# First stage of a cross-attention and expert kernel: a sum moved into PSUM, a norm moved to GpSimd, compares moved between VectorE's statistics

## The chip, the cores and the metric

The kernel runs on one core of a Trainium2 chip. The metric is the device time of one execution in microseconds (us). Before the change three runs took 929.35, 930.76 and 930.84 us, median 930.76.

A core has five engines that work at the same time, each through its own instructions in order: TensorE (PE in the profile: matrix products into PSUM; its weight loads are shown apart as PEld), VectorE (DVE), ScalarE (ACT: functions such as logarithm and exponential, also copies), GpSimd (POOL) and SyncE (SP: issues most DMAs here). An engine waits on a semaphore when its next instruction needs something that isn't there yet, and everything behind that instruction waits with it.

## What is computed

The reference is one transformer-like layer pair over `x` (32 x 56 x 256) and a context `ctx` (32 x 1500 x 256), all float32. Cut to what matters here:

```python
# first attention: a decayed scan over the context, averaged to one row per batch
s_t = K * s_{t-1} + (ctx_t @ W_in.T + b_in)         # K = sigmoid(decay)
summary = mean_t(s_t @ W_out.T + b_out)             # one row of 256 per batch
y  = layernorm(x) + summary
x  = x + (y - mean(y)) / sqrt(var(y) + eps) * gamma + beta
# first expert layer: 16 experts, the best 6 of each token
h = layernorm(x)
scores = softmax(h @ gate_w.T)
topk_w, topk_idx = top_k(scores, 6)
x = x + sum_e topk_w[e] * (silu(h @ wg[e].T) * (h @ wu[e].T)) @ wd[e].T
# second attention over ctx with a mask, then a layer of two experts
x = x + softmax(layernorm(x) @ ctx.T / 16, masked) @ ctx
x = x + top1_expert(layernorm(x))
return x
```

The change lies in the first stage: the first attention, the norm after it, the gate of the first expert layer, and the bookkeeping that sorts tokens by expert.

## The kernel before

The 32 batches are taken as 16 pairs (`NP = 16`). A pair's 2 x 56 tokens lie on the 128 partitions, batch 0 from partition 0 and batch 1 from partition 64, so that a pair is one tile of 128 x 256. The residual stream `xr` stays in SBUF for all pairs.

The context stands in a ring of five slots (`ring`, 1536 KB a batch). `load_ctx` (L145, issued by SP) fills a slot again as soon as `count_in` has read it.

The first stage's main loop is `for p in range(NP)` (L582). Its calls are written out by hand, and the order in which the calls stand is the order in which TensorE, VectorE, ScalarE and SP get their instructions; GpSimd's order is found by a scheduler. One round works on four pairs at once, each at another step:

- **Pair p, the summary.** `count_in` (L294) multiplies both batches' context by the scan's decay weights: 24 products of 32 columns each, accumulated in `acc`. `sum_out` (L408, ScalarE) copies it to SBUF; `sum_in_columns` (L414 on TensorE, L419 on VectorE) adds it up to columns, `sp` and then `sv`; `projected` (L427, then a ScalarE copy to `sm`, L431) applies the two weight matrices, multiplied beforehand; `to_rows` (L435) spreads the summary's rows over the 128 tokens, into `bp`.
- **Pair p-1, norms and gate.** `first_norm` adds `bp` to the normed input `zc` (L439), takes statistics (`stats`, L154 and L155) and lets ScalarE find the inverse root (`inverse_root`, L160 and L161: logarithm, then exponential). `residual` (L446, L447) applies it and takes the next statistics; `second_root` is the second inverse root; `second_norm` (L459, VectorE) makes the normed rows `xn`; `away` (L463, SP) stores them; `turned` (L166, L168) transposes them on TensorE and copies them to `xT`; `gate` (L471) gives 16 logits; `best` (a copy by ScalarE, L480, then L482 to L489 on VectorE, with an exponential, L491) marks the best six in `sel`.
- **Pair p-2, places.** `ranks` (L496, L497) counts, over tokens, how many chose each expert before; `counted` (L503, L504) turns that into positions; `places` (L510 to L526) splits a position into a block (`lvl`) and an offset (`off`), and prepares `vals`: the token's number and its weight for each expert and block. ScalarE makes the number half (L524). `ones_at` compares the offsets with 0 to 127, one 128 x 128 matrix per expert, 16 in all: twelve on VectorE in two instructions (L537, 1024 and 512 elements) and four on GpSimd (L543).
- **Pair p-3, sorting.** `sorted_in` (L562): 16 products on TensorE, of those matrices with `vals`, accumulated over all pairs in `owned`.

In every second round (p even, up to 12) `first_stats` (L393, L394 on VectorE and a root on ScalarE) and `first_rows` (L400, L404 on GpSimd: the normed input `zc`, and `beta` added to `xr`) prepare pairs p+2 and p+3.

In the order of before, `ones_at` stands at the end of a round, behind `best`, and `sorted_in` of the same pair follows in the next round. `first_stats` stands between `first_norm` and `residual`, `first_rows` behind `to_rows`. On TensorE a round is `count_in`, `sorted_in`, `ranks`, `sum_in_columns`, `turned`, `projected`, `gate`, `to_rows`. Six PSUM tiles a round go through a ring of five (`ps`).

After the loop, the last pairs are finished (L616 to L696) with `busy` (L552), products whose result nobody reads, in between; then the first expert layer begins with gathers of `xn` rows by GpSimd (L846).

Of the kernel before, what the change touches and what calls it, by code (L numbers as in the profile page):

```python
# [8 lines left out]
F32 = mybir.dt.float32  # L9
U8 = mybir.dt.uint8  # L10
I32 = mybir.dt.int32
AF = mybir.ActivationFunctionType
ALU = mybir.AluOpType
# [5 lines left out]
P = 128  # L19
B, S, D, T = 32, 56, 256, 1500  # L20
KD = D // P
NP = B // 2
# [6 lines left out]
NE = D // Q  # L29
CW = NCH * D  # L30
NRING, NXTRA = 5, 3
E0, F0, K0 = 16, 176, 6
# [22 lines left out]
def xattn_ffn_kernel(  # L55
# [94 lines left out]
    def stats(src):  # L150

        st = small.tile([P, 6], F32, tag="st", name="st")
        mv = small.tile([P, 4], F32, tag="mv", name="mv")
        V.bn_stats(out=st, in_=src)  # L154
        V.bn_aggr(out=mv[:, 0:2], in_=st)  # L155
        return mv
# [48 lines left out]
    with tc.tile_pool(name="p1", bufs=1) as p1, tc.tile_pool(name="p3", bufs=3) as p3, tc.tile_pool(  # L205
# [75 lines left out]
        def keep(p, **t):  # L281
            pend.setdefault(p, {}).update(t)

        def count_in(b):

            p, h = divmod(b, 2)
            if h == 0:
                keep(p, acc=psa.tile([P, 512], F32, tag="acc", name="acc"))
            acc = pend[p]["acc"]
            c = slots[b % NRING]  # L290
            for m in range(NCH // 4):
                for g in range(4):
                    j = 4 * m + g
                    PE.matmul(  # L294
                        acc[Q * g : Q * g + Q, 0:D],
                        lhsT=cz[:, j, 1 - h : 1 - h + Q], rhs=c[:, j, :],
                        start=(h == 0 and m == 0), stop=(h == 1 and m == NCH // 4 - 1),
                    )
            if b + NRING < B:
                load_ctx(b + NRING, c)  # L300
# [90 lines left out]
        def first_stats(o):  # L391
            for p in range(o, o + 2):
                V.bn_stats(out=st[:, p, :], in_=xr[:, p, :])  # L393
                V.bn_aggr(out=mva[:, p, :], in_=st[:, p, :])  # L394
            inverse_root(rsa[:, o : o + 2], mva[:, o : o + 2, 1])
# [10 lines left out]
        def sum_out(p):  # L406
            acc = p3.tile([P, D], F32, tag="acc", name="acc")
            A.copy(acc, pend[p]["acc"][:, 0:D])  # L408
            keep(p, acc=acc)

        def sum_in_columns(p):
            sp = ps.tile([P, 512], F32, tag="ps", name="sp")
            for k in range(KD):
                PE.matmul(  # L414
                    sp[:, 2 * k : 2 * k + 2], lhsT=pend[p]["acc"][:, k * P : (k + 1) * P],
                    rhs=sel2[:, 0:2], start=True, stop=True,
                )
            sv = p3.tile([P, KD, 2], F32, tag="sv", name="sv")
            V.tensor_scalar(  # L419
                sv.rearrange("p k h -> p (k h)"), sp[:, 0 : 2 * KD], 1.0 / T, None, ALU.mult  # L420
            )
            keep(p, sv=sv)

        def projected(p):
            sT = ps.tile([P, 512], F32, tag="ps", name="sT")
            for k in range(KD):
                PE.matmul(  # L427
                    sT[0:2, 0:D], lhsT=pend[p]["sv"][:, k, :], rhs=wc[:, k, :],
                    start=(k == 0), stop=(k == KD - 1),
                )  # L430
            A.copy(sm[0:2, :], sT[0:2, 0:D])  # L431

        def to_rows(p):
            bp = ps.tile([P, 512], F32, tag="ps", name="bp")
            PE.matmul(bp[:, 0:D], lhsT=takes, rhs=sm, start=True, stop=True)  # L435
            keep(p, bp=bp)

        def first_norm(p):
            V.tensor_tensor(zc[p], zc[p], pend[p]["bp"][:, 0:D], ALU.add)  # L439
            mv = stats(zc[p])  # L440
            inverse_root(mv[:, 2:3], mv[:, 1:2])
            keep(p, mv=mv)

        def residual(p):
            mv = pend[p]["mv"]
            V.scalar_tensor_tensor(zc[p], zc[p], mv[:, 0:1], gam, ALU.subtract, ALU.mult)  # L446
            V.scalar_tensor_tensor(  # L447
                xr[:, p, :], zc[p], mv[:, 2:3], xr[:, p, :], ALU.mult, ALU.add
            )
            keep(p, mv=stats(xr[:, p, :]))  # L450

        def second_root(p):
            mv = pend[p]["mv"]
            inverse_root(mv[:, 2:3], mv[:, 1:2])

        def second_norm(p):
            mv = pend[p]["mv"]
            xn = xnp.tile([P, D], F32, tag="xn", name="xn")
            V.tensor_scalar(xn, xr[:, p, :], mv[:, 0:1], mv[:, 2:3], ALU.subtract, ALU.mult)  # L459
            keep(p, xn=xn)  # L460

        def away(p):
# [37 lines left out]
        def counted(p):  # L500

            rk = pend[p]["rk"]
            V.tensor_tensor(pos[:, p, :], rk[:, 0:E0], base0, ALU.add)  # L503
            V.tensor_tensor(base0, base0, rk[:, E0 : 2 * E0], ALU.add)  # L504

        def places(p):

            nm, pr = pend[p]["nm"], pend[p]["pr"]
            qi = small.tile([P, E0], I32, tag="qi", name="qi")
            V.tensor_copy(qi, pos[:, p, :])  # L510
            V.tensor_scalar(qi, qi, 7, None, ALU.logical_shift_right)
            V.tensor_copy(lvl[:, p, :], qi)

            off = small.tile([P, E0], F32, tag="off", name="off")
            V.scalar_tensor_tensor(
                off, lvl[:, p, :], -float(P), pos[:, p, :], ALU.mult, ALU.add
            )
            V.scalar_tensor_tensor(off, off, 1.0, sel[:, p, :], ALU.add, ALU.mult)  # L518
            v = vals[:, p % 2]
            V.tensor_tensor(  # L520
                v[:, :, 1, :], e16.unsqueeze(1).to_broadcast([P, E0, NLP]),
                lvl[:, p, :].unsqueeze(2).to_broadcast([P, E0, NLP]), ALU.is_equal,
            )
            A.activation(v[:, :, 0, :], v[:, :, 1, :], AF.Copy, scale=ids[:, p : p + 1])  # L524
            V.reciprocal(nm[:, 1:2], nm[:, 1:2])
            V.scalar_tensor_tensor(  # L526
                v[:, :, 1, :], v[:, :, 1, :], nm[:, 1:2],
                pr.unsqueeze(2).to_broadcast([P, E0, NLP]), ALU.mult, ALU.mult,
            )
            keep(p, off=off)  # L530

        def ones_at(p):

            off = pend[p]["off"]
            hots = [at2.tile([P, NE, P], F32, tag="xq", name="oh") for h in range(2)]
            for h, n in ((0, NE), (1, NE // 2)):
                V.tensor_tensor(  # L537
                    hots[h][:, 0:n], iota.unsqueeze(1).to_broadcast([P, n, P]),
                    off[:, NE * h : NE * h + n].unsqueeze(2).to_broadcast([P, n, P]),
                    ALU.is_equal,  # L540
                )
            for i in range(NE // 2, NE):
                G.tensor_scalar(  # L543
                    hots[1][:, i, :], iota, off[:, NE + i : NE + i + 1], None, ALU.is_equal
                )
            keep(p, hots=hots)

        def busy(n):

# [32 lines left out]
        for p in range(NP):  # L582
            if p >= 1:
                first_norm(p - 1)
            if p % 2 == 0 and p + 2 < NP:
                first_stats(p + 2)
            if p >= 1:
                residual(p - 1)
                count_in(2 * p)
                second_root(p - 1)  # L590
                count_in(2 * p + 1)
            sum_out(p)
            if p >= 3:
                sorted_in(p - 3)
            if p >= 2:
                ranks(p - 2)
            if p >= 1:
                second_norm(p - 1)
                away(p - 1)
                some_pieces(1)  # L600
            sum_in_columns(p)
            if p >= 1:
                turned(p - 1)
            projected(p)
            if p >= 2:
                counted(p - 2)
                places(p - 2)
            if p >= 1:
                gate(p - 1)
            to_rows(p)  # L610
            if p % 2 == 0 and p + 2 < NP:
                first_rows(p + 2)
            if p >= 1:
                best(p - 1)
            if p >= 2:
                ones_at(p - 2)  # L616
            if p == NP - 3:
                load_w0_up()
            if p > NP - 3:
                some_pieces(6)  # L620
        first_norm(NP - 1)
        sorted_in(NP - 3)
        ranks(NP - 2)
        busy(2)
        residual(NP - 1)
        second_root(NP - 1)
        second_norm(NP - 1)
        away(NP - 1)
        some_pieces(len(pieces))
# [3 lines left out]
        gate(NP - 1)  # L633
        busy(1)
        best(NP - 1)
        ones_at(NP - 2)
        ranks(NP - 1)
        sorted_in(NP - 2)
        counted(NP - 1)
# [21 lines left out]
            )  # L661
        busy(2)
        places(NP - 1)
        ones_at(NP - 1)
        blk = p2.tile([P, 4], F32, name="blk")
        V.tensor_copy(blk, bp[:, 0:4])
        hot = slots[B % NRING].rearrange("p j d -> p (j d)")
# [704 lines left out]
```

## Time and profile before

| what | us |
|---|---|
| runs | 929.35, 930.76, 930.84; median 930.76 |
| the profiled execution, whole | 928.71 |
| its span | 927.0 |
| start of the span to the loop's first `first_norm` | 0 to 38.5 |
| loop, L439's first to last start | 38.5 to 200.1 |
| last pairs, to the first gather of the expert layer | 200.1 to 223.4 |
| the rest: both expert layers and the second attention | 223.4 to 927.0 |

Busy time of each engine by stretch of the span (us):

| stretch | length | PE | DVE | ACT | POOL | granted PE clock | DMA share | GB/s |
|---|---|---|---|---|---|---|---|---|
| 0 to 38 | 38.0 | 19.1 | 11.8 | 4.9 | 17.5 | 0.92 | 0.96 | 307 |
| 38 to 200 | 162.0 | 138.0 | 120.2 | 47.5 | 61.1 | 0.77 | 0.88 | 315 |
| 200 to 223.4 | 23.4 | 20.2 | 15.3 | 3.4 | 7.7 | 0.66 | 0.19 | 56 |
| 223.4 to 489 | 265.6 | 255.1 | 87.8 | 119.4 | 142.1 | 0.98 | 0.52 | 157 |
| 489 to 927 | 438.0 | 400.1 | 250.2 | 177.6 | 153.8 | 0.96 | 0.49 | 162 |

How to read the profile: the span is the time from the first to the last recorded instruction of one execution. A line of the timeline has start, duration, engine, line of the program, operation, what it writes `<-` what it reads, the shape, and how often it ran in a row; in brackets stand the idle time of the engine before it and who ended that. A line of the waits has who waited, for whom, and then the microseconds in total, the number of times and the longest. The granted clock is the share of its full clock that TensorE was given. Matmul ends are modelled, so a busy TensorE is not a TensorE at its peak.

### The profile page before, as it was taken

To read this page: it belongs to the slowest core of one execution; us is meant where nothing else is said; L and a number is where in the kernel's file an instruction comes from. 1 tells how busy PE (TensorE), PEld (TensorE's weight loads), DVE (VectorE), ACT (ScalarE), POOL (GpSimd) and SP (SyncE) were. 2 spreads that over 40 slices of the span, in tenths; PEclk is the share of its full clock that TensorE was granted. 3 is DMA by queue.
4 is the path that set the end of the run, shared out by engine and by line. 5 is a ranking of instruction groups with operands and counts; after the bars stand their busy time and mean duration, and the time that the engine had idled before them with its cause. 6 is when DMAs were issued, how large, how long until landed. Compare 5 with 4: busy or idle time off the path is not lost.

```text
span 927.0 us, 18683 instructions
## 1 busy us (share of the span) xinstructions
PE 832.5 (90%) x6664; PEld 539.8 (58%) x6664; DVE 485.3 (52%) x1409; ACT 352.8 (38%) x921; POOL 382.3 (41%) x464
## 2 busy tenths in 40 slices
PE   4698888887999898999996999987968989999997
PEld 4355444444777676777773566554635546666664
DVE  3377777774563222232227789977848533332222
ACT  0222222321444545444444575774734421111111
POOL 4333344335437545556633645664560321111110
PEclk9777777777999999999997999998998999999999
DMA  9998878881797624344537687888862911011110
GB/s 284 354 386 305 316 291 326 267 230 32 243 319 232 185 90 123 94 137 119 137 87 235 230 279 258 267 289 263 307 229 98 339 60 35 23 35 30 35 35 17
DMA packets 77820, 176.58 MB, mean 190 GB/s; under 512 B 7795, under 2 KB 41476, under 8 KB 77732
## 3 DMA queue, kind: packets, MB, share of 16 engines
q1 hardware_dynamic: 64756, 139.55, 43.7%
q0 software_dynamic: 12976, 35.85, 13.5%
q8 instruction: 56, 0.92, 0.4%
q14 instruction: 32, 0.26, 0.1%
HBM read 150.83 MB, written 25.20 MB: 190 GB/s over the span
## 4 chain that ended last, share of the span: by engine, by line
PE 44%; POOL 11%; DMA 9%; issue 6%; DVE 3%; ACT 2%; POOLq 0%; ACTq 0%; DVEq 0%
PE gu L714 22%; PE y L741 14%; DMA g<-ys,back 8%; POOL g L776 6%; PE tp L732 4%; PE tp L166 3%; POOL g L786 2%; PE op L1053 1%; DVE cT L966 1%; POOL g L788 1%; POOL g L787 1%; DMA xs<-pay,to 1%; PE sp L1005 1%; POOL xr L789 1%; POOL xs L1144 0%
## 5 line engine op out<-in xcount | busy, mean ns | idle before, releaser
L714 PE MATMUL gu<-w_sb,xT 128*128 x396 | 136.7, 467 | 8.8 <-ACT xT L168 7.6
L720 ACT ACTIVATE sg<-gu 128x176 f32<-128x176 f32 (+1 forms) x159 | 54.3, 342 | 216.7 <-PE gu L714 216.6
L846 POOL DMA_INDIRECT xb<-xn,idx x99 | 93.8, 947 | 100.1 <-PE tp L166 83.7
L726 DVE SCALAR_TENSOR_TENSOR hs<-sg,wgt,gu 128x176 f32<-128x176 f32 x99 | 39.3, 397 | 174.0 <-ACT sg L720 174.0
L714 PE MATMUL gu<-ring,xT 128*128 x240 | 114.2, 599 | 0.5 <-ACT xT L168 0.5
L776 POOL DMA_INDIRECT g<-ys,back x96 | 91.0, 948 | 33.2 <-issue 25.8
L741 PE MATMUL y<-w_sb,hT 88*128 x396 | 102.7, 382 | 0.0
L1005 PE MATMUL sp<-cT,xq 32*64 32x384 f32 x2048 | 94.2, 512 | 3.4 <-DVE cT L966 3.3
L714 PEld LDWEIGHTS gu<-w_sb,xT 128*128 128x128 f32 x396 | 74.8, 191 | 37.7 <-ACT xT L168 11.0
L724 DVE TENSOR_TENSOR hs<-sg,gu 128x256 f32<-128x256 f32 x60 | 25.2, 421 | 117.1 <-ACT sg L720 117.1
L966 DVE STREAM_TRANSPOSE cT<-ring 128x1536 f32<-128x1536 f32 x40 | 69.3, 1760 | 18.8 <-PE sp L1005 10.7
L732 PEld LDWEIGHTS tp<-ident,hs 128*88 128x88 f32 (+1 forms) x318 | 41.4, 131 | 63.2 <-issue 49.1
L1053 PE MATMUL op<-ring,pT 128*64 128x256 f32 x480 | 67.8, 396 | 9.2 <-issue 9.2
L543 POOL TENSOR_SCALAR oh<-iota,off 128x128 f32<-128x128 f32 x64 | 41.7, 665 | 80.3 <-DVE off L518 72.9
L1005 PEld LDWEIGHTS sp<-cT,xq 32*64 32x64 f32 x2048 | 45.4, 140 | 44.4 <-issue 17.6
L741 PEld LDWEIGHTS y<-w_sb,hT 88*128 88x128 f32 x396 | 67.9, 191 | 5.7 <-issue 0.2
L1307 POOL DMA_INDIRECT out<-ob,ti x15 | 14.8, 988 | 131.4 <-DVE ob L1304 131.4
L168 ACT COPY xT<-tp 128x256 f32<-128x256 f32 x130 | 48.4, 372 | 52.6 <-PE tp L166 51.6
L734 DVE COPY hT<-tp 88x256 f32<-88x256 f32 (+1 forms) x159 | 66.0, 415 | 0.6 <-PE tp L732 0.6
L714 PEld LDWEIGHTS gu<-ring,xT 128*128 128x128 f32 x240 | 45.6, 191 | 33.1 <-issue 29.4
L732 PE MATMUL tp<-ident,hs 128*88 128x128 f32 (+1 forms) x318 | 61.5, 276 | 2.6 <-DVE hs L724 2.6
L294 PE MATMUL acc<-ring,cz 128*32 128x256 f32 x768 | 62.9, 493 | 0.2 <-DVE cz L270 0.2
(258 smaller groups left out, 1361.2 us busy)
## 6 DMA issues: line engine op xcount, KB each, us to landing
ring<-in_cx SPq DMA_DIRECT2D x52, 1536.0 KB
extra<-in_cx SPq DMA_DIRECT2D x12, 1536.0 KB
ys<-yb SPq DMA_DIRECT2D x99, 128.0 KB
xs<-zrow SPq DMA_DIRECT2D x5, 771.0 KB
mu<-in_mask SPq DMA_DIRECT2D x16, 187.5 KB
w_sb<-in_wg SPq DMA_DIRECT2D x2, 1408.0 KB
w_sb<-in_wu SPq DMA_DIRECT2D x2, 1408.0 KB
xn<-xn SPq DMA_DIRECT2D x16, 128.0 KB
```

The lines of the kernel that those rows point to most:

```text
L168: A.copy(xT.rearrange("p k c -> p (k c)"), tp[:, 0 : KD * P])
L294: PE.matmul(acc[Q * g : Q * g + Q, 0:D], lhsT=cz[:, j, 1 - h : 1 - h + Q], rhs=c[:, j, :], start=(h == 0 and m == 0), stop=(h == 1 and m = ...
L714: PE.matmul(gu[:, 0 : 2 * fp], lhsT=xT[i][:, k, :], rhs=w[:, bass.ds(at[i] + (u * piece + k * 2 * fp), 2 * fp)], start=(k == 0), stop=(k = ...
L720: A.activation(sg, gu[:, 0:fp], AF.Silu)
L732: PE.transpose(tp[0:h, c * P : (c + 1) * P], a[:, c * h : (c + 1) * h], ident)
L734: V.tensor_copy(hT[i, u], tp[0:h, 0 : 2 * P])
L741: PE.matmul(y[i][:, 0:D], lhsT=a[:, c * P : (c + 1) * P], rhs=w[0:h, bass.ds(at[i] + (u * piece + doff + c * D), D)], start=(u == 0 and c ...
L776: G.indirect_dma_start(out=g[:, k, :], out_offset=None, in_=ys0[0 : n * P, :], in_offset=bass.IndirectOffsetOnAxis(ap=back[:, p, 3 * i + k ...
L846: G.indirect_dma_start(out=xb, out_offset=None, in_=xn0, in_offset=bass.IndirectOffsetOnAxis(ap=idx[:, i : i + 1], axis=0),)
L966: V.transpose(out=cT.rearrange("p j e q -> p j (e q)"), in_=slots[b % NS][:, :, P * n : P * n + P],)
L1005: PE.matmul(sps[a][64 * h : 64 * h + 64, 0 : Q * NCH], lhsT=xq[Q * a : Q * a + Q, e, 64 * h : 64 * h + 64], rhs=cTs[e // 4][h][Q * a : Q * ...
L1053: PE.matmul(op[64 * h : 64 * h + 64, 0:D], lhsT=pT[:, j, 64 * h : 64 * h + 64], rhs=slots[(2 * p + h) % NS][:, j, :], start=(j == 0), stop ...
```

## The change

1. The summary's rows are added to `zc` on TensorE: `to_rows` first multiplies `zc` by the identity into `bp`, then accumulates the rows on top. VectorE's add (L439) goes; the statistics and L446 read `bp` in PSUM.
2. `second_norm` runs on GpSimd, except for the last pair.
3. In `places`, ScalarE's scale (L524 before) stands after VectorE's product and works in place; the product no longer waits for it.
4. `ones_at` is split in two halves and moved by a round: for pair p-3, the first half behind `first_norm`, the second behind `residual`, in the round in which `sorted_in(p-3)` runs.
5. The order of the calls: `sum_out` before `second_root`; `counted` right behind `sum_in_columns`; `projected` before `turned`; `first_stats` from behind `first_norm` to behind `to_rows`; `first_rows` behind `best`.

```diff
         def to_rows(p):
             bp = ps.tile([P, 512], F32, tag="ps", name="bp")
-            PE.matmul(bp[:, 0:D], lhsT=takes, rhs=sm, start=True, stop=True)
+            PE.matmul(bp[:, 0:D], lhsT=ident, rhs=zc[p], start=True, stop=False)
+            PE.matmul(bp[:, 0:D], lhsT=takes, rhs=sm, start=False, stop=True)
             keep(p, bp=bp)
 
         def first_norm(p):
-            V.tensor_tensor(zc[p], zc[p], pend[p]["bp"][:, 0:D], ALU.add)
-            mv = stats(zc[p])
+            mv = stats(pend[p]["bp"][:, 0:D])
             inverse_root(mv[:, 2:3], mv[:, 1:2])
             keep(p, mv=mv)
 
         def residual(p):
             mv = pend[p]["mv"]
-            V.scalar_tensor_tensor(zc[p], zc[p], mv[:, 0:1], gam, ALU.subtract, ALU.mult)
+            V.scalar_tensor_tensor(
+                zc[p], pend[p]["bp"][:, 0:D], mv[:, 0:1], gam, ALU.subtract, ALU.mult
+            )
...
-            V.tensor_scalar(xn, xr[:, p, :], mv[:, 0:1], mv[:, 2:3], ALU.subtract, ALU.mult)
+            (V if p == NP - 1 else G).tensor_scalar(
+                xn, xr[:, p, :], mv[:, 0:1], mv[:, 2:3], ALU.subtract, ALU.mult
+            )
...
             V.tensor_tensor(
-                v[:, :, 1, :], e16.unsqueeze(1).to_broadcast([P, E0, NLP]),
+                v[:, :, 0, :], e16.unsqueeze(1).to_broadcast([P, E0, NLP]),
                 lvl[:, p, :].unsqueeze(2).to_broadcast([P, E0, NLP]), ALU.is_equal,
             )
-            A.activation(v[:, :, 0, :], v[:, :, 1, :], AF.Copy, scale=ids[:, p : p + 1])
             V.reciprocal(nm[:, 1:2], nm[:, 1:2])
             V.scalar_tensor_tensor(
-                v[:, :, 1, :], v[:, :, 1, :], nm[:, 1:2],
+                v[:, :, 1, :], v[:, :, 0, :], nm[:, 1:2],
                 pr.unsqueeze(2).to_broadcast([P, E0, NLP]), ALU.mult, ALU.mult,
             )
+            A.activation(v[:, :, 0, :], v[:, :, 0, :], AF.Copy, scale=ids[:, p : p + 1])
...
+        def ones_at(p, h):
+            off = pend[p]["off"][:, NE * h : NE * h + NE]
+            oh = at2.tile([P, NE, P], F32, tag="xq", name="oh")
+            n = NE // 2 if h else NE
+            V.tensor_tensor(
+                oh[:, 0:n], iota.unsqueeze(1).to_broadcast([P, n, P]),
+                off[:, 0:n].unsqueeze(2).to_broadcast([P, n, P]), ALU.is_equal,
+            )
+            for i in range(n, NE):
+                G.tensor_scalar(oh[:, i, :], iota, off[:, i : i + 1], None, ALU.is_equal)
+            pend[p].setdefault("hots", []).append(oh)
...
         for p in range(NP):
             if p >= 1:
                 first_norm(p - 1)
-            if p % 2 == 0 and p + 2 < NP:
-                first_stats(p + 2)
+            if p >= 3:
+                ones_at(p - 3, 0)
             if p >= 1:
                 residual(p - 1)
+            if p >= 3:
+                ones_at(p - 3, 1)
+            if p >= 1:
                 count_in(2 * p)
-                second_root(p - 1)
                 count_in(2 * p + 1)
             sum_out(p)
+            if p >= 1:
+                second_root(p - 1)
             if p >= 3:
                 sorted_in(p - 3)
...
             sum_in_columns(p)
+            if p >= 2:
+                counted(p - 2)
+            projected(p)
             if p >= 1:
                 turned(p - 1)
-            projected(p)
             if p >= 2:
-                counted(p - 2)
                 places(p - 2)
             if p >= 1:
                 gate(p - 1)
             to_rows(p)
             if p % 2 == 0 and p + 2 < NP:
-                first_rows(p + 2)
+                first_stats(p + 2)
             if p >= 1:
                 best(p - 1)
-            if p >= 2:
-                ones_at(p - 2)
+            if p % 2 == 0 and p + 2 < NP:
+                first_rows(p + 2)
...
         first_norm(NP - 1)
+        ones_at(NP - 3, 0)
+        residual(NP - 1)
+        ones_at(NP - 3, 1)
+        second_root(NP - 1)
         sorted_in(NP - 3)
         ranks(NP - 2)
         busy(2)
-        residual(NP - 1)
-        second_root(NP - 1)
         second_norm(NP - 1)
```

As built, GpSimd's order in the changed loop is: the four compares of pair p-3, the second norm of pair p-1, and in even rounds the two norms and two adds of `first_rows` behind that. ScalarE's order from the transposes on is: the copy to `xT`, the scale of `places`, the roots of `first_stats` in even rounds, the copy of the logits.

## The prediction

> **What bounds the kernel now.** The change touches only the first stage, which the table of stretches puts at 0 to 223.4 us of the 927.0 us span; its loop (rounds p = 0 to 15) runs from 38 to 200 us. I asked first for the waits in that loop.
>
> ```profile
> DVE sv L419 <- PE sp L414: 12.0, 12, 1.9
> DVE vals L526 <- ACT vals L524: 9.1, 14, 0.9
> DVE xn L459 <- ACT mv L161: 9.0, 15, 0.6
> DVE xr L447 <- ACT mv L161: 0.5, 1, 0.5
> ```
>
> VectorE (DVE) is busy 120.2 of these 162 us, and most of the rest is these waits. The second root costs it 0.6 us in each round (L459); the first root costs nothing except once (L447), because L446 runs under it. The loads are not the bound; in the queue's own waits between 80 and 172 us the context loads stand for a free slot:
>
> ```profile
> SPq L145 <- PE acc L294: 56.5, 17, 6.6
> ```
>
> Then one round on VectorE, from the timeline (start, duration, line):
>
> ```profile
> 180.08 0.41 DVE L439 TENSOR_TENSOR z<-z,bp 128x256 f32<-128x256 f32 x1
> ...
> 181.20 0.48 DVE L446 SCALAR_TENSOR_TENSOR z<-z,mv,gam 128x256 f32<-128x256 f32 x1
> 181.79 0.48 DVE L447 SCALAR_TENSOR_TENSOR xr<-z,mv,xr 128x256 f32<-128x256 f32 x1
> ...
> 183.55 0.41 DVE L459 TENSOR_SCALAR xn<-xr,mv 128x256 f32<-128x256 f32 x1 [0.60 <-ACT mv L161]
> 184.47 0.16 DVE L419 TENSOR_SCALAR sv<-sp 128x4 f32<-128x4 f32 x1 [0.51 <-PE sp L414]
> ...
> 186.75 0.51 DVE L526 SCALAR_TENSOR_TENSOR vals<-vals,nm,pr 128x256 f32<-128x256 f32 x1 [0.50 <-ACT vals L524]
> ...
> 188.09 1.81 DVE L537 TENSOR_TENSOR oh<-iota,off 128x1024 f32<-128x1024 f32 x2
> 189.82 0.41 DVE L439 TENSOR_TENSOR z<-z,bp 128x256 f32<-128x256 f32 x1
> ```
>
> A round is one pass over VectorE, 9.74 us here. The compares (L537) stand at its end, where TensorE already counts the next pair: they lie beside `count_in`. The sixteen L439 starts give rounds of 9.74 to 10.25 us without L393's statistics, 11.1 us where `count_in` ran at half clock, and 11.5 to 11.8 us with them; rounds 5 to 15 take 200.07 - 81.38 = 118.7 us.
>
> TensorE's timeline shows the clock:
>
> ```profile
> 183.83 0.61 PE L414 MATMUL sp<-sel,acc 128*128 128x2 f32 x4 [2.42 <-ACT acc L408]
> ...
> 187.95 4.88 PE L294 MATMUL acc<-ring,cz 128*32 128x256 f32 x48
> 192.66 1.05 PE L562 MATMUL owned<-oh,vals 128*32 128x128 f32 x32
> ```
>
> After 2.42 us idle the count takes 4.88 us instead of 2.80 (granted clock 0.50 at 190 us).
>
> **The change, part by part.** Times are counted from F, the start of VectorE's first statistics in a round, in start-to-start steps of the round above.
>
> *Sum in PSUM.* Removes L439 (0.44). TensorE gets one 128x256 matmul, bounded by half of L427's two (0.96/2 = 0.48). The statistics and L446 now read PSUM: no row of either from there; L439 with PSUM takes 0.41 where L393 without takes 0.40, so 0 +- 0.05. The bank is held until L446 (F+2.4); its next taker in the ring of five, the logits, comes at F+7.9: nothing.
>
> *Norm on GpSimd.* Removes L459 and its wait (0.41 + 0.60). GpSimd pays L400's price for the same form, 1.25, after the root at F+4.2: done near F+5.6. TensorE's transposes now stand behind `projected`, so they ask later (F+7.0): covered by that, and 1.25 us on the path if it were not. The store `away` leaves about 1 us later; behind it in SP's queue are a weight piece and the next loads, which wait for a slot anyway: nothing.
>
> *Scale after the product.* L526 loses its 0.50 wait. But ACT's queue now reads scale, [roots of `first_stats`], copy of the logits, and `best` waits for that copy: scale to logits 0.42, copy to L482 0.22, 0.67 in all. The wait is moved, not filled. In rounds with statistics the roots (0.57) stand there instead: 0.8 us.
>
> *Compares moved.* They leave the end of the round, where they covered `count_in`, for places ahead of `sorted_in` of the same round. On TensorE `sorted_in` stands before `ranks` and `sp`, so VectorE's `sv` now waits for its own compares through TensorE. Walk at full clock: first statistics 0.68; first half of the compares 1.15 (to 1.83); L446, L447 1.11 (2.94); statistics 0.67 (3.61); second half 0.58 (4.19). TensorE: half of `sorted_in` 0.55, `ranks` 0.47, sp to sv 0.64: sv at 5.85, so VectorE idles 1.66. `counted` and `places` 2.22 (8.07), the ACT wait 0.67, `best` 0.90: **9.64**. TensorE's side (sT 0.96, transposes 0.39, copy 0.48, logits 0.55, sum 0.48 + 0.74) ends at 9.67, level with it. With statistics 1.06 and 0.8 for 0.67: **10.8**.
>
> *GpSimd's queue.* This decides. Its order becomes: `first_rows` (two norms, two adds), four compares, second norm.
>
> ```profile
> 72.38 1.39 POOL L400 TENSOR_SCALAR z<-xr,mva,rsa 128x256 f32<-128x256 f32 x1 [4.25 <-ACT rsa L161]
> ...
> 75.91 0.74 POOL L404 TENSOR_TENSOR xr<-xr,bet 128x256 f32<-128x256 f32 x1
> ...
> 87.48 2.37 POOL L543 TENSOR_SCALAR oh<-iota,off 128x128 f32<-128x128 f32 x4 [7.55 <-DVE off L518]
> ```
>
> `first_rows` now starts at the end of an even round, after the statistics' roots, 1.0 us before the next F; alone it took 2.41 + 1.40 = 3.81 (at 36.18 and 38.57 us). So it ends at F+2.8, and the compares, which TensorE's last four `sorted_in` matmuls need, at F+5.16 instead of 4.19: the odd round grows by about 0.75, to 10.4. But VectorE's two-input operations now run beside it, and a row shows that price:
>
> ```profile
> 215.02 1.81 DVE L537 TENSOR_TENSOR oh<-iota,off 128x1024 f32<-128x1024 f32 x2
> ...
> 215.03 2.18 POOL L543 TENSOR_SCALAR oh<-iota,off 128x128 f32<-128x128 f32 x1
> 217.20 1.41 POOL L543 TENSOR_SCALAR oh<-iota,off 128x128 f32<-128x128 f32 x1
> ```
>
> A compare that takes GpSimd 0.59 took 2.18 beside VectorE's compares. If GpSimd loses all of 1.15, 0.48 (L447) and 0.58 us, it is done at F+7.4 and the odd round is **12.6**. Bounds 10.4 and 12.6; I take 12.6, as that row is the nearest. The Trainium skill's page "SBUF — State Buffer", section "Who interferes with whom", says whichever engine holds the shared port first blocks the other for the whole instruction, where VectorE reads two SBUF inputs. The row agrees when VectorE came first; but L537 at 67.83 us began inside a GpSimd compare (65.76 to 68.13) and still took 1.81. By the page VectorE would wait as well, up to 1.25 us more in each such round; the sum leaves that out.
>
> *Clock.* In those rounds TensorE idles most of F+2.6 to F+7.4. Idle of 1.89 (before 51.64 us), 2.42 and 3.3 us was followed each time by half clock. Lower bound 0. Upper: everything from `sorted_in` to the sum at half clock (sT 1.86, transposes 0.65, logits 1.04, takes 1.22, the steps before +1.0), 3.5 per odd round. I take 1.3, what half clock cost before (sv waited 1.8 to 1.9 us instead of 0.5 to 0.67). The count of the next round at half clock, 4.9 us from the sum's end, ends about when the second compares do: covered. The skill's "TensorE: Matmul & The Clock Gate", section "HAM oscillation — how this bites in real kernels", asks for idle over about 3.4 us; the 2.42 us row halved the clock sooner. By the page the walk without GpSimd's stretch would pay nothing.
>
> *Sum.* Rounds 5 to 15: 5 odd x 12.6 + 4 even x 10.8 + 2 plain x 9.64 + 5 x 1.3 = 132.0, against 118.7: +13.3. Rounds 1 to 4: round 1 the same (it starts 0.85 earlier, since the roots of pairs 2 and 3 no longer stand before `sum_out`, and gives that back by the later transposes); round 2 has no compares, 8.6 against 11.5; round 3 13.9 against 11.1; round 4 10.8 against 11.8: -1.1. Tail: pair 13's compares move behind the last first norm, so from the last sum's start to the last transposes it is 0.74 to F, 4.2 to the compares' end, then by the rows from 199.69 us 0.95 (half of `sorted_in`), 0.88 and 3.5 (`busy`): 10.3 against 205.94 - 196.45 = 9.5, +0.8. Together +13.0. The profiled execution took 928.7 us (1.7 of it outside the span), 2 under the median of 930.8, so 941.7 to 943.8: **943**. No term stands for the rest of the kernel, from 223 us on: its instructions are the same.
>
> **Rivals.** (1) *GpSimd is late but not stretched*, clock as priced: odd rounds 10.4, so 11 less in rounds 5 to 15 and 2.2 in round 3: -0.2, 930. For it: the four compares mostly kept 2.37 in the loop; against: they then met no VectorE compare. (2) *Faster: the clock stays full.* TensorE's idle ahead of `sorted_in` shrinks below what halves the clock, and GpSimd is not stretched: also 1.3 x 6 less, -8.0, 922. It decides from an idle of about 1.2 us (halfway: 0.5 before 43.42 us changed nothing, 1.89 did). The walk has 1.66 even in the good rounds, which speaks against it. (3) *Half clock through the whole odd round*: 3.5 in place of 1.3 six times, +13 more: 956. For it: a gap of 4 us is longer than any of before. (4) *Loads bind instead*: against, the 56.5 us wait for slots.
>
> **Chances.** Forecast 0.50, (1) 0.18, (2) 0.14, (3) 0.16, (4) 0.02. Range 928 to 958: from just below (1) to (3), leaving out (2) and little above. Under 0.2% (1.9 us) the measurement can't tell from no change. Faster: (2) and a third of (1), 0.20; same: half of (1), 0.09; slower 0.71.
>
> **What would show it.** Right: `sv` waits 1.7 us or more for sp in every round, `sorted_in`'s last matmuls wait for GpSimd in odd rounds, L400 or the compare on GpSimd stretches over VectorE's compares, L482 waits 0.7 for ACT, half clock in odd rounds. Wrong: `sv`'s wait stays under 1 us, GpSimd done before F+5, or granted clock above the 0.77 of before in the loop.

## The result and the profile after

| | before | after |
|---|---|---|
| runs, us | 924.64 to 930.84, median 930.06 | 956.02, 960.45, 960.67, 965.16, median 960.56 |
| profiled execution / its span | 928.71 / 927.0 | 965.16 / 963.4 |

The ratio is 1.0341, 95% interval 1.0278 to 1.0404: slower, as forecast, but above the range of 928 to 958. The profiled execution after is the slowest of its four, so the pair of traces is 36.4 us apart in span and the medians 30.5.

Where the 36.4 us lie, by the starts of `first_norm`'s statistics (loop), and the first gather (end of the tail):

| stretch | before | after | difference | forecast |
|---|---|---|---|---|
| start to the first statistics | 38.47 | 38.80 | +0.3 | 0 |
| rounds 1 to 4 | 42.9 | 49.0 | +6.1 | -1.1 |
| rounds 5 to 15 | 118.7 | 139.0 | +20.3 | +13.3 |
| tail, to the first gather | 23.3 | 28.1 | +4.75 | +0.8 |
| the rest | 703.6 | 708.6 | +5.0 | 0 |

No instruction of the rest is changed; its 5.0 us is of the size by which runs of one kernel differ (956 to 965), and I explain the other 31.

Rounds 1 to 15 after: 11.54, 10.58, 14.59, 12.25, 14.11, 11.04, 14.90, 11.72, 14.64, 12.17, 14.19, 10.96, 14.91, 10.67, 9.66 us. Odd rounds from 3 to 13 take 14.1 to 14.9 us (before 9.85 to 11.15), even ones 11 to 12.3.

The waits of the loop after, 38 to 226 us (who waited for whom; total, times, longest):

```profile
DVE sv L419 <- PE sp L414: 43.8, 15, 3.6
DVE m L486 <- ACT lg L484: 21.3, 15, 3.2
PE owned L563 <- DVE oh L541: 14.7, 8, 2.2
```

VectorE's wait for `sp` has grown from 12.0 to 43.8 us, and the wait for the logits from 1.9 (once) to 21.3 us. In the next view, busy time by stretch (length; PE, PEld, DVE, ACT, POOL with counts; granted clock, DMA share, GB/s), the loop grew from 162 to 188 us at the same mean clock:

```profile
38.00:226.00 188.00, 158.81 (x1462) 86.78 (x1461) 105.52 (x381) 47.52 (x174) 80.83 (x98) 0.77 0.77 275
226.00:254.80 28.80, 23.38 (x149) 14.46 (x149) 17.27 (x55) 3.84 (x13) 8.11 (x13) 0.59 0.10 29
```

VectorE's work fell to 105.5 us, and yet the stage is longer: no engine's work became the bound. The DMA share fell from 0.88 to 0.77, so it isn't the loads. One odd round from the timeline, F = 112.91:

```profile
113.46 1.43 DVE L541 TENSOR_TENSOR oh<-iota,off 128x1024 f32<-128x1024 f32 x1
...
115.04 0.65 PE L563 MATMUL owned<-oh,vals 128*32 128x128 f32 x16 [0.45 <-ACT acc L408]
115.40 1.05 DVE L449 SCALAR_TENSOR_TENSOR xr<-z,mv,xr 128x256 f32<-128x256 f32 x1
116.15 2.71 POOL L546 TENSOR_SCALAR oh<-iota,off 128x128 f32<-128x128 f32 x4
...
117.87 0.87 PE L563 MATMUL owned<-oh,vals 128*32 128x128 f32 x14 [2.18 <-DVE oh L541]
118.92 0.64 PE L563 MATMUL owned<-oh,vals 128*32 128x128 f32 x2 [0.17 <-POOL oh L546]
...
120.36 0.99 PE L414 MATMUL sp<-sel,acc 128*128 128x2 f32 x4
121.39 0.16 DVE L419 TENSOR_SCALAR sv<-sp 128x4 f32<-128x4 f32 x1 [3.57 <-PE sp L414]
121.61 1.87 PE L427 MATMUL sT<-wc,sv 128*2 128x256 f32 x4 [0.25 <-DVE sv L419]
...
124.56 1.03 PE L475 MATMUL lp<-gw_sb,xT 128*128 128x16 f32 x4 [0.46 <-ACT xT L168]
...
125.83 0.18 DVE L486 MAX8 m<-lg 128x8 f32<-128x16 f32 x1 [2.14 <-ACT lg L484]
...
127.71 5.04 PE L294 MATMUL acc<-ring,cz 128*32 128x256 f32 x48
```

`sorted_in` (L563) stands ahead of `sp` on TensorE. It waits 2.18 us for VectorE's second compares and 0.17 for GpSimd's. From about 118.8 us on, everything on TensorE takes nearly double: `sp` 0.99 for 0.61, `sT` 1.87 for 1.02, the logits 1.03 for 0.62. The same round cut there, again by stretch:

```profile
112.90:118.80 5.90, 3.21 (x62) 1.68 (x54) 4.64 (x9) 1.39 (x6) 5.90 (x8) 0.99 1.03 358
118.80:126.60 7.80, 6.96 (x23) 3.99 (x23) 2.74 (x17) 1.62 (x6) 3.67 (x6) 0.50 0.68 265
```

Full clock until 0.9 us behind the wait, half from there on. The count of the next round, at 127.71, still took 5.04 us instead of 2.80, so that the even round starts late too.

### The profile page after: what moved, and what is told of

The parts are those of the page before. It is cut to its first block, busy times and chain, and to the rows that moved or that the text cites. A ratio compares the mean times of both kernels' runs of the same rounds, so it can differ in the third digit from the quotient of the medians.

```text
span 963.4 us, 18725 instructions
## 1 busy us (share of the span) xinstructions
PE 858.5 (89%) x6696; PEld 550.0 (57%) x6696; DVE 473.7 (49%) x1378; ACT 353.1 (37%) x921; POOL 402.1 (42%) x479
## 4 chain that ended last, share of the span: by engine, by line
PE 44%; POOL 11%; DMA 9%; issue 6%; ACT 1%; DVE 1%; POOLq 0%; ACTq 0%; DVEq 0%
PE gu L724 21%; PE y L751 13%; DMA g<-ys,back 8%; POOL g L786 5%; PE tp L742 3%; PE tp L166 3%; POOL g L796 2%; PE op L1063 2%; PE sp L1015 1%; POOL g L797 1%; POOL g L798 1%; DMA xs<-pay,to 1%; POOL xr L799 1%; PE tp L1055 0%; POOL xs L1154 0%
## 5 line engine op out<-in xcount | busy, mean ns | idle before, releaser
L724 PE MATMUL gu<-w_sb,xT 128*128 x396 | 139.0, 474 | 8.8 <-ACT xT L168 7.6
L1063 PEld LDWEIGHTS op<-ring,pT 128*64 128x64 f32 x480 | 41.4, 142 | 35.9 <-issue 13.8
L751 PE MATMUL y<-ring,hT 128*128 x240 | 61.7, 380 | 0.0
```

The costliest lines, as they stand in the source:

```text
L724: PE.matmul(gu[:, 0 : 2 * fp], lhsT=xT[i][:, k, :], rhs=w[:, bass.ds(at[i] + (u * piece + k * 2 * fp), 2 * fp)], start=(k == 0), stop=(k = ...
L751: PE.matmul(y[i][:, 0:D], lhsT=a[:, c * P : (c + 1) * P], rhs=w[0:h, bass.ds(at[i] + (u * piece + doff + c * D), D)], start=(u == 0 and c ...
L1063: PE.matmul(op[64 * h : 64 * h + 64, 0:D], lhsT=pT[:, j, 64 * h : 64 * h + 64], rhs=slots[(2 * p + h) % NS][:, j, :], start=(j == 0), stop ...
```

## The experiments

The theory: `sorted_in`, standing ahead of `sp` on an engine that works in order, makes TensorE idle; the idle halves its clock, and the half clock is the loss. Rivals: GpSimd's late compares, GpSimd's norm, VectorE's waits themselves. The first eight ran where the kernel before takes 927 to 929 us. The later seven ran where it takes 988.4 and 986.7; the extra lies behind the first gather (766 us from there to the end in one of them, 704 in the trace of before), so rounds and first gathers can be compared, times only by ratio. Ratios are to the kernel before, measured along with each. "First gather" is at 223.4 us before and at 254.8 after.

**1. Only `sorted_in` moved.**

```diff
-            if p >= 3:
-                sorted_in(p - 3)
...
             projected(p)
+            if p >= 3:
+                sorted_in(p - 3)
             if p >= 1:
                 turned(p - 1)
```

> The changed kernel with sorted_in of pair p-3 moved on TensorE from before ranks to behind projected, so that sp and sv no longer stand behind VectorE's compares. Theory C (TensorE idles about 2.2 us ahead of sorted_in while VectorE compares, falls to half clock, and the rest of the round runs at half clock): the idle ahead of sorted_in goes, the odd rounds fall from 14.1-14.9 us to about 11, the time from 960 to 930-940 us. Theory G (GpSimd's second norm and its collisions with VectorE are the cost): no more than 3 us of change, 957-961 us.

Measured 922.83 us, ratio 0.9961 (0.9932 to 0.9991): one call moved takes back the whole loss and a little more, better than the 930 to 940 expected. Odd rounds 9.94, even ones 10.54, first gather at 217.05. An odd round in its timeline, and the loop by stretch:

```profile
140.91 2.80 PE L294 MATMUL acc<-ring,cz 128*32 128x256 f32 x48
...
144.20 0.61 PE L414 MATMUL sp<-sel,acc 128*128 128x2 f32 x4
144.54 2.71 POOL L546 TENSOR_SCALAR oh<-iota,off 128x128 f32<-128x128 f32 x4
146.33 0.81 PE L427 MATMUL sT<-wc,sv 128*2 128x256 f32 x3 [1.52 <-DVE sv L419]
...
147.19 1.04 PE L563 MATMUL owned<-oh,vals 128*32 128x128 f32 x26
...
148.52 0.44 PE L166 MATMUL tp<-ident,xn 128*128 128x128 f32 x2 [0.29 <-POOL xn L461]
```

```profile
38.00:190.00 152.00, 130.69 (x1462) 77.37 (x1461) 107.97 (x381) 47.04 (x174) 80.78 (x98) 0.90 0.94 335
```

GpSimd's compares take the same 2.71 us and end as late (F+5.95); now only `sorted_in` needs them, and nothing urgent stands behind it. The clock rises to 0.90 and the DMA share to 0.94: the loads are close to being the bound.

**2 and 3. The gap filled.** Products on constants, whose results nobody reads: first two of 512 columns ahead of `sorted_in`, then one ahead of its first half, and in odd rounds two between the halves.

```diff
+            d = psa.tile([P, 512], F32, tag="acc", name="d")
+            for _ in range(n):
+                PE.matmul(d, lhsT=ident, rhs=wc.rearrange("p k d -> p (k d)"), start=True, stop=True)
...
-                sorted_in(p - 3)
+                warm(1)
+                sorted_in(p - 3, range(0, NE))
+                if p % 2:
+                    warm(2)
+                sorted_in(p - 3, range(NE, E0))
```

> The changed kernel with two products of 512 columns on constant data put on TensorE between count_in and sorted_in (1.9 us at full clock; their result is not read), nothing else moved. If the half clock is what makes the moved compares dear: the loop's granted clock rises from 0.76 to over 0.9, odd rounds fall from 14.5 to 11-12 us, the time to 935-945 us although TensorE has more to do. If the order alone (full-clock chain) is the cost, the added products change nothing or add up to 10 us: 960-970 us.

> The changed kernel with the sorting products cut in halves and filling products of 512 columns around them (one before the first half, two between the halves in odd rounds), whose results nobody reads. Clock theory (the loss is TensorE's idle ahead of and between the halves, which halves the clock for the rest of the round): odd rounds fall from 14.5 us to 11-11.5, granted clock of the loop from 0.77 to 0.87 or more, time 935-942. Rival (the loss is the waits themselves, GpSimd's compares and VectorE's, with full clock or not): odd rounds stay at 13.5 or more, time 950 or more.

The first: 954.51 us, ratio 1.0311 (1.0262 to 1.036), above the 935 to 945 expected. The gap between the halves was still 0.78 us, and odd rounds from 5 on (13.85) still fell to half clock; even rounds took 13.3, with the added products behind a count that ran in part at half clock. But its round 3, with a gap of 0.92 us, kept the full clock and took 11.32 us, where round 5 took 13.97 with the same work in the same order. The two rounds, 3 and 5:

```profile
62.03 0.87 PE L571 MATMUL owned<-oh,vals 128*32 128x128 f32 x14 [0.92 <-DVE oh L541]
...
64.71 1.02 PE L427 MATMUL sT<-wc,sv 128*2 128x256 f32 x4 [0.26 <-DVE sv L419]
...
84.84 0.87 PE L571 MATMUL owned<-oh,vals 128*32 128x128 f32 x14 [0.78 <-DVE oh L541]
...
87.65 1.87 PE L427 MATMUL sT<-wc,sv 128*2 128x256 f32 x4 [0.25 <-DVE sv L419]
```

The second: ratio 1.0133 (1.0076 to 1.019), first gather 231.3, the loop's clock 0.94. The timeline of one of its odd rounds:

```profile
105.47 1.12 PE L562 MATMUL d<-wc,ident 128*128 128x512 f32 x2
106.52 0.65 PE L571 MATMUL owned<-oh,vals 128*32 128x128 f32 x16
107.09 1.98 PE L562 MATMUL d<-wc,ident 128*128 128x512 f32 x4
109.01 0.69 PE L571 MATMUL owned<-oh,vals 128*32 128x128 f32 x14
109.87 0.41 PE L571 MATMUL owned<-oh,vals 128*32 128x128 f32 x2 [0.17 <-POOL oh L546]
...
111.52 1.02 PE L427 MATMUL sT<-wc,sv 128*2 128x256 f32 x4 [0.26 <-DVE sv L419]
...
115.07 2.80 PE L294 MATMUL acc<-ring,cz 128*32 128x256 f32 x48
```

GpSimd's compares end as late as after the change (F+5.97) and VectorE's too; only the idle is filled, and the clock stays up. This round takes 11.33 us in place of 14.1 to 14.9, even rounds 10.67. In two odd rounds (5 and 11) the count in front ran at half clock after all, 5.12 and 4.76 us, and those took 13.98 and 13.67. So the order of the work is the smaller cost, and the clock the larger. By the ratio its time is some 941 us where the kernel before takes 928.6, at the upper end of the expected 935 to 942; those two rounds, the filling itself and the tail stay.

**4, 5 and 6. One part of the change undone.** Compares back behind `best`; the second norm on VectorE (`V.tensor_scalar` for all pairs); `first_stats` and `first_rows` back.

```diff
-                ones_at(p - 3, 0)
...
-                ones_at(p - 3, 1)
...
                 first_rows(p + 2)
+            if p >= 2:
+                for h in range(2):
+                    ones_at(p - 2, h)
```

> The changed kernel with the compares back where they were (both halves of pair p-2 at the end of the round); the sum in PSUM, the norm on GpSimd, the late scale and the other orders stay. Theory C: nearly all of the loss goes, 925-938 us. Theory G: the norm is still on GpSimd, the loss stays for the most part, 950-960 us.

> The changed kernel with the second norm on VectorE for every pair again. Theory C: the norm on GpSimd was off the path; VectorE gets 0.41 us more per round at a place where it idles 2-3 us for sp, so 957-963 us, no change. Theory G: 935-948 us.

> The changed kernel with first_stats and first_rows at their old places; the compares stay where the change put them. Theory (each late step alone is enough to halve the clock, and the compares ahead of sorted_in stay late): 935-950, odd rounds (no first_rows beside the compares) 10-11, even rounds 12.5 or more, because GpSimd takes the second norm behind the two norms. Rival (the old places of first_rows alone cure it): 930 or less, all rounds under 11.5.

Compares back: 961.41, ratio 1.0393 (1.0342 to 1.0444), no gain at all: a miss. Norm on VectorE: 955.78, ratio 1.0339 (1.0261 to 1.0417) against 1.0341, no difference beyond that interval; GpSimd's norm is not the cost. Rows back: ratio 1.0206 (1.0153 to 1.0259), some 12 us of the loss gone, odd rounds 10.5, even ones 13.4, as expected. What TensorE waited for, in the first and in the third:

```profile
143.77 0.41 PE L563 MATMUL owned<-oh,vals 128*32 128x128 f32 x2 [2.68 <-POOL oh L546]
```

```profile
148.35 0.64 PE L563 MATMUL owned<-oh,vals 128*32 128x128 f32 x16 [1.72 <-DVE oh L541]
...
150.24 1.85 PE L427 MATMUL sT<-wc,sv 128*2 128x256 f32 x4 [0.26 <-DVE sv L419]
```

With the compares back, `first_rows` stands in front of GpSimd's four compares and delays them by itself. With the rows back, TensorE still waits for VectorE's compares in every even round; in the odd ones the count in front runs at half clock (4.9 us) and ends behind them. Either way a gap of 1.7 to 2.7 us stays ahead of `sp` in every second round, and half clock follows it.

**7. Both undone.**

> The changed kernel with the compares back at the end of the round AND first_stats and first_rows back at their old places; sum in PSUM, norm on GpSimd, late scale, sum_out before second_root and projected before turned stay. Theory S (whatever makes sorted_in late holds up TensorE ahead of sp; there are two such things, VectorE's compares in the same round and GpSimd's compares behind first_rows, and each alone is enough to halve the clock): both gone, 920-930 us, odd rounds near 10 us. Theory R (some of the parts that stay is the cost): 945-960 us.

939.27, ratio 1.0102 (1.008 to 1.0124): most of the loss gone, but not all, a miss again. GpSimd's order, which a scheduler finds, now puts both norms of `first_rows` ahead of `xn`, and TensorE's transposes wait for that in even rounds (12.9 us):

```profile
131.81 0.69 PE L166 MATMUL tp<-ident,xn 128*128 128x128 f32 x2 [3.45 <-POOL xn L461]
```

**8 to 10. One part of the change alone**, put into the kernel before: the compares; `first_stats` and `first_rows`; the sum in PSUM. The edits are those of the change's diff.

> The kernel before with one part alone: the compares moved as in the change (two halves between VectorE's statistics, in the round of their sorted_in). Theory S: TensorE idles 2 us and more ahead of sorted_in in every round, the clock halves, 945-960 us, most of the change's loss from this part alone. Theory R: under 935 us.

> The kernel before with one part alone: first_stats behind to_rows and first_rows behind best, so that GpSimd's four compares stand behind first_rows. Theory S: sorted_in waits over 2 us for GpSimd in every odd round, odd rounds near 14 us, 940-955 us. Theory R: under 935 us.

> The kernel before with one part alone: the summary added to zc on TensorE, VectorE's add gone. By the walk VectorE saves 0.44 us in each of 15 rounds where VectorE is the bound and TensorE pays 0.5 us where it is not: 6 us less, 920-925 us. If TensorE's extra product counts instead (half clock, 1.2 us): 928-935 us.

| part alone | time, us | ratio | first gather |
|---|---|---|---|
| compares | 938.55 | 1.0098 (1.0076 to 1.0119) | 237.0 |
| `first_stats`, `first_rows` | 948.18 | 1.0221 (1.0172 to 1.0271) | 244.8 |
| sum in PSUM | 925.61 | 0.9961 (0.994 to 0.9982) | 221.5 |

Only the rows came as theory S expected; the compares lie between its 945 and theory R's 935, and the sum gained half of the 6 us of its walk. With the compares alone `sorted_in` waits twice in an even round, for VectorE; with the rows alone it waits for GpSimd:

```profile
143.40 0.64 PE L559 MATMUL owned<-oh,vals 128*32 128x128 f32 x16 [1.88 <-DVE oh L537]
146.00 1.08 PE L559 MATMUL owned<-oh,vals 128*32 128x128 f32 x16 [1.96 <-DVE oh L537]
```

```profile
139.94 2.40 PE L562 MATMUL owned<-oh,vals 128*32 128x128 f32 x8 [2.98 <-POOL oh L543]
```

Against the 928.62 us of before the three alone add up to 9.9 + 19.6 - 3.0 = 26.5 us, near the whole 30.5. They add because they lie in different rounds: the compares alone lengthen the even ones (13.4 us for 11.5 to 11.8), the rows alone the odd ones (13.8 for 9.9 to 11.2). They don't subtract in the same way: each late part alone opens a gap, so that taking one out of the whole leaves the other's.

**11. The tail.** Only the order behind the loop put back; the compares and `sorted_in` of pair 13 stand behind the last `second_norm` and the last `gate`.

```diff
         first_norm(NP - 1)
-        ones_at(NP - 3, 0)
+        ranks(NP - 2)
+        busy(2)
         residual(NP - 1)
-        ones_at(NP - 3, 1)
         second_root(NP - 1)
-        sorted_in(NP - 3)
-        ranks(NP - 2)
-        busy(2)
         second_norm(NP - 1)
...
+        ones_at(NP - 3, 0)
+        ones_at(NP - 3, 1)
         turned(NP - 1)
...
         gate(NP - 1)
+        sorted_in(NP - 3)
```

> The changed kernel with only the order behind the loop put back: the compares and the sorting products of the last odd pair but one stand behind the last second norm and behind the last gate, the loop stays as changed. Theory: the change costs 4.75 us from the last first statistics to the first gather (23.3 to 28.1), since these compares (1.85 us) and sorting products stand on the last pair's path; put back, this stretch falls to 23.5-25 and the time by 3.5-4.5 us, to 0.4% under the changed kernel's ratio of 1.034, so about 1.030. Rival (the stretch is longer because TensorE's clock is half anyway): 27 us or more, ratio unchanged.

Ratio 1.0284 (1.0235 to 1.0333). From the last statistics to the gather 23.96 us in place of 28.1, as the theory had it; the ratio itself is not clear of the 1.0341 (1.0278 to 1.0404) of the change. TensorE after the change, and TensorE and VectorE here:

```profile
228.64 1.08 PE L563 MATMUL owned<-oh,vals 128*32 128x128 f32 x16 [1.94 <-DVE oh L541]
230.86 1.08 PE L563 MATMUL owned<-oh,vals 128*32 128x128 f32 x16 [1.13 <-DVE oh L541]
...
232.74 3.76 PE L553 MATMUL d<-ring,ident 128*128 128x512 f32 x4
236.29 0.63 PE L166 MATMUL tp<-ident,xn 128*128 128x128 f32 x2
```

```profile
226.88 3.41 PE L553 MATMUL d<-ring,ident 128*128 128x512 f32 x4
...
229.22 0.41 DVE L461 TENSOR_SCALAR xn<-xr,mv 128x256 f32<-128x256 f32 x1 [0.60 <-ACT mv L161]
229.55 1.82 DVE L541 TENSOR_TENSOR oh<-iota,off 128x1024 f32<-128x1024 f32 x2
230.13 0.38 PE L166 MATMUL tp<-ident,xn 128*128 128x128 f32 x2
```

After the change the filling products stood behind two waits, and the last transposes behind them.

**12 to 15. Towards a better version.** The changed kernel with `sorted_in` late, VectorE's second compares behind `sv`, the logits' copy ahead of the roots and the scale behind `best`; the same with only `sorted_in` late and the old tail; the kernel before with three gains (sum in PSUM, `sum_out` ahead of `second_root`, scale behind `best`); and that without the move of `sum_out`. The third, beside the sum's edit:

```diff
                 count_in(2 * p)
-                second_root(p - 1)
                 count_in(2 * p + 1)
             sum_out(p)
+            if p >= 1:
+                second_root(p - 1)
...
-            A.activation(v[:, :, 0, :], v[:, :, 1, :], AF.Copy, scale=ids[:, p : p + 1])
...
             if p >= 2:
+                numbers(p - 2)
                 ones_at(p - 2)
```

> The changed kernel with sorted_in behind projected, VectorE's second compares behind sv, the copy of the logits ahead of the first roots and the scale behind best. If the order on TensorE alone was the cost, the rest saves VectorE's remaining waits: rounds 9.4-9.7 us, time 912-918. Rival (with sorted_in behind projected the rounds already stand at the loads' floor of some 9.1 to 9.9 us): 919-925, no better than moving sorted_in alone (922.8), with the loop's DMA share at 0.95 or more.

> The changed kernel with sorted_in behind projected in the loop and the old order behind it. If the loop and the tail are separate costs, both gains add up: first gather at 213-214.5 us (217.05 with the loop alone), ratio to the kernel before 0.991-0.993. Rival (the shorter tail is paid back by compares that run later): gather at 216 or more, ratio 0.996.

> The kernel before with three parts of the change only: the sum in PSUM, sum_out before second_root, and the scale placed behind best. Each takes work off VectorE's path without making TensorE's sorted_in wait. Theory: 918-922. Rival (VectorE's time was not what set the plain rounds): 925 or more, no better than the sum alone (925.6).

> The kernel before with the sum in PSUM and the scale behind best, without moving sum_out. Theory: in the version with sum_out moved the odd rounds took 10.84 us, because VectorE's norm waits 2.6 us for a root that stands behind sum_out and a count at half clock; without that move odd rounds take 10.2 or less, even ones 9.7-10.2, first gather at 211-213, ratio 0.985-0.99. Rival (the move of sum_out is itself a gain in every round): rounds of 10.5 and more, gather at 215 or more, ratio above 0.99.

| version | ratio | first gather |
|---|---|---|
| changed, three further moves | 1.0068 (1.0038 to 1.0098) | 224.8 |
| changed, `sorted_in` late, old tail | 0.9972 (0.9935 to 1.0009) | 218.3 |
| before, three gains | 0.9899 (0.9862 to 0.9936) | 215.0 |
| before, without the move of `sum_out` | 0.9965 (0.9925 to 1.0005) | 215.65 |

The first lost: with the copy ahead of the roots, `first_rows` starts later on GpSimd, `xn` follows at F+7.2 instead of 5.95, and the transposes wait 0.82 us for it (odd rounds 11.2 to 11.8). The second has the shorter tail (23.95 us) but was no faster than experiment 1: its rounds 1, 7 and 9 took 11.59, 10.89 and 11.90 us in place of some 9.9. Its trace is of an execution of 992.2 us where the median is 982.4, so whether the two cures add up stays open. The third beats both kernels, inside what was expected of it (918 to 922 of 930 is 0.987 to 0.991). Its odd rounds, whose count runs at half clock, take 10.84, its even ones 9.70 (in an execution of 988.7 us; the median is 979.4). The fourth missed its 0.985 to 0.99; the intervals of the two overlap, so that it is weaker isn't shown.

## Why the prediction was wrong

The sign and the place were right; the sum was 13.0 us where 30.5 (medians) came. In the pair of traces 31.4 us lie up to the first gather, 18.4 more than forecast: 7.2 in rounds 1 to 4, 7.0 in rounds 5 to 15, 3.9 in the tail and 0.3 ahead of the loop.

- **What failed: the step *Clock*.** I priced half clock at 1.3 us in each odd round, between bounds of 0 and 3.5, and nowhere else. Experiment 2/3 measures it: with the same lateness at full clock an odd round takes 11.33 us and not 14.1 to 14.9, so about 3.2, near the upper bound (rival 3's 3.5). And it spreads: "the count of the next round at half clock ... covered" is wrong. In even rounds VectorE's second compares were done at F+4.07, the count at F+4.2 to 5.25, and `sorted_in` and `sp` follow the count; even rounds took 11.0 to 12.3 for the 10.67 of experiment 3. Of the 7.0 us that rounds 5 to 15 exceed the forecast, 3.2 lie in the five odd rounds, 2.7 in the even ones, and 1.0 in round 14 (count 5.00 us). With experiment 3's full-clock rounds, 5 x 11.33 + 4 x 10.67 + 2 x 9.66 = 118.7, just what rounds 5 to 15 took before. So all of the +20.3 us there is the clock (the filling's own time is in these rounds, so if anything more).
- **The walk at full clock was right.** Plain 9.64 forecast, 9.66 measured (round 15, where `sv` waited 1.72 us for a forecast 1.66); with statistics 10.8, measured 10.67 (experiment 3). On TensorE's side the terms written add up to 9.45; the 9.67 takes in 0.22 us from `sv`'s start to `sT`.
- **GpSimd's queue: too much on GpSimd, nothing on VectorE.** I took 2.2 us per odd round for compares stretched by VectorE. They took 2.71 for 2.39 us and ended at F+5.95, 0.8 behind the unstretched F+5.16, and TensorE waited 0.17 for them. VectorE, which the sum let off, was held up about as long beside L400 and L404: its first compares 1.43 us for 1.19, L449 1.05 for 0.48, together 0.8. That is the direction which the Trainium skill's "SBUF — State Buffer", section "Who interferes with whom", gives (VectorE waits as well), though by less than a whole instruction of GpSimd: one norm of L400 takes 1.21 us here. A delay of 0.8, on either engine, brings the unstretched 10.4 to 11.2, against 11.33. So 1.3 too much here and 1.9 too little in the clock nearly cancelled in odd rounds (13.9 forecast, 14.5 measured on average): that their sum came close is luck.
- **Rounds 1 to 4, -1.1 forecast, +6.1 measured.** Rounds 1 and 2 took 11.54 and 10.58 for 8.5 and 8.6; with the same loop in experiment 11 they took 9.72 and 8.84. So some 3.5 us of this is where the half clock fell in this execution (the loop as a whole took 187.9 and 188.0 us in the two).
- **Tail: my sum counted from two points.** The rounds end at the last statistics, but the +0.8 was counted from the last sum, 2.9 us earlier relative to them in the kernel before (3.62 against 0.73). From the sum's start to the last transposes I forecast 10.3, and 10.29 came; from the last statistics it is 9.56 against 5.87, so +3.7 belonged in the sum. Another 1.06 came from the transposes to the gather.
- **Sum in PSUM, the norm, the scale.** The sum alone is worth 3.0 us. The norm on GpSimd shows no cost (experiment 5, to some 0.8% either way). The moved wait for the logits was 0.63 to 0.66 us at full clock, as forecast (0.67; 0.8 with statistics), and 2.15 in odd rounds, where half clock made the logits late.
- **Rivals.** Rival 2 named the right hinge: held near full clock, the loop costs nothing. Rival 3 was what happened in odd rounds, and I gave it 0.16 because I kept what half clock had cost before. The mean clock of the loop is 0.77 before and after; if it is either full or half, some 75 of 162 us and 86 of 188 us ran at half clock (an estimate from these shares). So it matters more where half clock falls than how much of it there is: before, on a count with VectorE's compares and norms beside it; after, on `sp`, `sT` and the logits, for which VectorE waits. Loads (rival 4) did not bind.

On the rule of the skill: "TensorE: Matmul & The Clock Gate", section "HAM oscillation — how this bites in real kernels", was weighed by its 3.4 us, which by the page would have cost nothing here. The runs speak against using it as a limit: in each odd round from 3 to 13 a wait of 2.18 to 2.20 us was followed by half clock. The page's next section, "A second HAM failure mode: psum-queue depth-cycling", tells of a kernel whose short, frequent idles make the clock swing; that is nearer to what these runs show.

## What to carry to other kernels

- On an engine that works in order, look for what stands behind a product that waits. Bookkeeping whose result nobody needs soon belongs behind the work that the critical chain needs; moving one call took back the whole loss (experiment 1).
- Price a new TensorE wait by the clock that follows it, through the rest of the round and the next long accumulation, not by its own length; here that came near the upper bound, because nothing hid it.
- Parts that each open a gap at the same place don't subtract: undone one at a time, one gave back nothing (experiment 4) and the other 12 of some 31 us (experiment 6). And count every stretch of a sum from the same instruction in both kernels.

## What was unexpected of the hardware

Half clock outlasted its cause: from 0.9 us after a wait of 2.18 us the granted clock was 0.50 for 7.8 us, with TensorE busy for 6.96 of them, and the count behind that still took 5.04 us for 2.80. No length of gap decides it: about 1.0 us ahead of the second half of `sorted_in` left round 15 at full clock after the change, and was followed by half clock (a sum product of 1.22 us for 0.69) in experiment 11; 0.78 us in experiment 2 was followed by half clock, in a stretch with other gaps of 0.17 and 0.26 and products of 2 to 32 columns, and 0.92 us two rounds earlier was not. What the clock counts stays open.
